# A cross-attention block on one core: context before the low scores, turned weights on two queues, SyncE in written order

## The chip, the cores and the metric

The kernel runs on one core of one Trainium2 chip, as one launch. The time is in device microseconds (us). The core has TensorE (PE; its weight loads are shown as PEld), VectorE (DVE), ScalarE (ACT), GpSimd (POOL), SyncE (SP), which issues transfers, and 16 DMA engines that move them. ScalarE has a DMA queue of its own (ACTq), SyncE another (SPq). Issuing a transfer takes time on the engine that issues it.

## The reference

One transformer block with cross attention, in float32, over 128 sequences of 128 tokens with 256 features; 16 heads of 16, a hidden layer of 1024. `query` is x, `key` and `values` are both the context. Token i sees context tokens j < i, so token 0 sees nothing and its attention weights are set to zero.

```python
q = (query @ Wq + bq)...; k = (key @ Wk + bk)...; v = (values @ Wv + bv)...   # split into 16 heads
scores = jnp.einsum('bhqd,bhkd->bhqk', q, k) / jnp.sqrt(jnp.float32(D_K))
allowed = j < i + mask                                   # mask = 0
scores = jnp.where(allowed, scores, NEG_INF)
attn = jax.nn.softmax(scores, axis=-1)
attn = attn.at[:, :, 0, :].set(0.0)
ctx = jnp.einsum('bhqk,bhkd->bhqd', attn, v)
attn_out = ctx @ Wo + bo
x = layer_norm(query + attn_out, ln1_g, ln1_b)
ffn = jax.nn.relu(x @ W1 + b1) @ W2 + b2
out = layer_norm(x + ffn, ln2_g, ln2_b)
```

## The kernel before

The 128 sequences are taken two at a time: 64 pairs, numbered p. Loop step p (L790) is a software pipeline over four pairs. It makes the scores and the softmax of pair p, the attention output and first normalization of pair p - 1, the hidden layer of pair p - 2 and the second product of pair p - 3, and it projects queries, keys and values of pair p + 1. Pairs 0 and 1 are done ahead of the loop, steps 2 to 5 have a filling order of their own (`plan`), and the last step and the lines after the loop drain it.

Tokens 64 to 127 of a sequence are called high and see up to 128 context tokens; tokens 0 to 63 are low and see at most 64. `scores` makes 32 small matmuls (32 rows, 64 columns of the array) for each part, with 256 streamed columns for high and 128 for low, into the two PSUM buffers of `ps_2`, which both parts use in turn. `mask` (VectorE) reads them from there, in two halves for each part, so a part's scores wait for the masks of the part before. Then the softmax passes between engines: `maximum` (VectorE, then a subtraction on GpSimd, L354), `exponential` (ScalarE, L361), `sums` (VectorE, then a multiplication on GpSimd, L375). The high part goes through maximum, exponential and sums in two halves of eight heads (ONE and TWO), the low part at once (ALL).

To multiply with the values, the weights have to be turned. `turn` transposes 32 x 32 blocks on VectorE into `tb` (three instructions, two for high and one for low), and 16 transfers on SyncE's queue (L401, 96 KB each) bring the blocks to their partitions in `pT`. Both tiles have one buffer. `weigh(p)` multiplies `pT` with the values (96 small matmuls, 128 rows and 32 columns, into `pc`; L434, L444), `context` copies the result (ScalarE, L456), `attention_out` multiplies with Wo. `turn_x1` turns the normalized x in the same way, by five transfers through DRAM (`x1t`, `x1T`), for `hidden`. Before `weigh`, `values_out` (ScalarE) copies the values to `vz` and sends a part of them by a transfer of its own to `vd` (L305).

The bank pool `ps_1` has four PSUM buffers, used in the order py (second product), pc, pq (queries), po (attention output), pk (keys), pv (values), and four ph (hidden, two chunks of the hidden layer each). `hidden` is evicted by ScalarE (`hT`, L615, two instructions for each ph); `second` makes 16 matmuls for each sequence of the pair. `finish`, `norm2` and `store` complete the second normalization, one step later.

The order on PE, DVE, ACT and POOL is the order in which the lines are written (`manual_schedule`, L60). SyncE's order is left to the framework, which interleaves loads and other transfers as it plans them. In the written order of one step TensorE does: high scores, second product of the first sequence, low scores, second product of the second sequence, weigh, queries, attention output, keys, values, hidden. Loads of the transposed blocks `xb` and `cb` (four transfers for two pairs) and of the tokens `x` (three buffers) stand near the end of a step (L843).

Each transfer signals one of eight semaphores, which the framework gives out in turn over both queues; a transfer waits until the earlier one with the same semaphore has landed, where that is not known already.

Of the kernel before, what the change touches and what calls it, by code (L numbers as in the profile page):

```python
# [8 lines left out]
F32 = mybir.dt.float32  # L9
# [4 lines left out]
P = 128  # L14
# [5 lines left out]
def tile_cross_attention_block(  # L20
# [36 lines left out]

    ET = mybir.EngineType
    ctx.enter_context(
        tc.manual_schedule(engines={ET.PE, ET.DVE, ET.Activation, ET.Pool})  # L60
    )

    const = ctx.enter_context(tc.tile_pool(name="const", bufs=1))
# [16 lines left out]
    def load(ps, both="xc"):  # L80

        n = len(ps)
        for which in both:
            src = x if which == "x" else c
            t = loads.tile(
                [P, KC, n * 2 * NS, 32], F32, tag=f"{which}b{n}", name=f"{which}b_{ps[0]}",
                bufs=n,
            )
            blocks = src[2 * ps[0] : 2 * ps[0] + 2 * n].rearrange(
                "b (i t) (k j f) -> j t k (b i) f", t=32, k=KC, f=32  # L90
            )
            for j in range(NS):
                nc.sync.dma_start(t[32 * j : 32 * j + 32], blocks[j])  # L93
            for u, p in enumerate(ps):
                blocks_of[which, p] = t[:, :, u * 2 * NS : (u + 1) * 2 * NS]

    def load_tokens(g, us=slice(0, 4)):
        if g not in tokens_of:
            tokens_of[g] = loads.tile([P, 4, D], F32, tag="x", name=f"x_{g}")
        nc.sync.dma_start(  # L100
            tokens_of[g][:, us], x[4 * g + us.start : 4 * g + us.stop].rearrange("b p d -> p b d")
        )
# [162 lines left out]
    def queries(p):  # L265
        st = states[p]
        st["qT"] = proj.tile([P, KC, TP], F32, tag="qT", name=f"qT_{p}")
        pq = project(wq, st["xT"], f"pq_{p}")
        for m in range(KC):
            nc.scalar.activation(  # L270
                st["qT"][:, m, :], pq[:, m * TP : (m + 1) * TP], AF.Identity,
                bias=bqs_c[:, m : m + 1], scale=QSCALE,
            )
# [41 lines left out]
    def scores(p, hi):  # L315

        st = states[p]
        n = P if hi else HP
        sps = [pair(f"pss{hi}_{p}_{t}") for t in range(2)]
        for m in range(KC):  # L320
            for s in range(2):
                first = s * P
                for r in range(NS):
                    strip = slice(32 * r, 32 * r + 32)
                    nc.tensor.matmul(  # L325
                        sps[r // 2][
                            s * HP : (s + 1) * HP, r % 2, m * 2 * n : (m + 1) * 2 * n
                        ].rearrange("p (e j) -> p e j", e=2),
                        st["qT"][strip, m, first + hi * HP : first + hi * HP + HP],
                        st["kT"][strip, m, :, first : first + n],  # L330
                        start=True, stop=True,
                    )
        st["sps", hi] = sps
        st["sm", hi] = soft.tile([P, H, n], F32, tag=f"sm{hi}", name=f"sm{hi}_{p}")
        st["nmx", hi] = small.tile([P, H], F32, tag=f"nmx{hi}", name=f"nmx{hi}_{p}")
# [43 lines left out]

    def turn(p):


        st = states[p]
        tb = soft.tile([P, NS, (H + HH) * 32], F32, tag="tb", name=f"tb_{p}")
        at = 0
        for hi in (1, 0):
            sm = st["sm", hi].rearrange("p h j -> p (h j)")
            for t in range(sm.shape[1] // 1024):  # L390
                nc.vector.transpose(  # L391
                    tb[:, :, at : at + 256].rearrange("p j (n a) -> p n j a", a=32),
                    sm[:, t * 1024 : (t + 1) * 1024].rearrange(
                        "p (n j a) -> p n j a", j=NS, a=32
                    ),
                )
                at += 256
        pT = soft.tile([P, NS, (H + HH) * 32], F32, tag="pT", name=f"pT_{p}")
        for i in range(NS):
            for j in range(NS):  # L400
                nc.sync.dma_start(  # L401
                    pT[32 * j : 32 * j + 32, i, :], tb[32 * i : 32 * i + 32, j, :]
                )
        st["pT"] = pT.rearrange("p i (n a) -> p i n a", a=32)

    def turn_on_pe(p, hi, ts):

# [63 lines left out]
    def stats(p, t, i):  # L471
        st = states[p]
        mv = st["mv", i] = small.tile([P, 2, 2], F32, tag=f"mv{i}", name=f"mv{i}_{p}")
        for s in range(2):
            bs = small.tile([P, 6], F32, tag="bs", name=f"bs{i}_{p}_{s}", bufs=4)
            nc.vector.bn_stats(bs, t[:, s])
            nc.vector.bn_aggr(mv[:, s], bs)
# [8 lines left out]
    def attention_sum(p):  # L486
        st = states[p]
        t1 = st["t1"] = ffn.tile([P, 2, D], F32, tag="t1", name=f"t1_{p}")
        nc.vector.tensor_tensor(
            t1, st.pop("po").rearrange("p (s d) -> p s d", s=2), st.pop("xb"), ALU.add  # L490
        )
        stats(p, t1, 1)
        deviation(p, 1)

    def norm1(p):
# [102 lines left out]
        for k in range(KC):  # L598
            nc.scalar.copy(st["x1T"][:, :, :, k, :], pt[:, k])  # L599

    def hidden(p, fs):
        st = states[p]
        if fs[0] == 0:
            st["hT"] = ffn.tile([P, FC, TP], F32, tag="hT", name=f"hT_{p}")
        for f in fs[::2]:
            ph = bank(f"ph_{p}_{f}")
            for i in range(2):
                for k in range(KC):
                    nc.tensor.matmul(  # L609
                        ph[:, i * TP : (i + 1) * TP].rearrange("p (s i a) -> p s i a", s=2, a=32),  # L610
                        w1[:, k, (f + i) * P : (f + i + 1) * P], st["x1T"][:, :, :, k, :],
                        start=(k == 0), stop=(k == KC - 1),
                    )
            for i in range(2):
                nc.scalar.activation(  # L615
                    st["hT"][:, f + i, :], ph[:, i * TP : (i + 1) * TP], AF.Relu,
                    bias=b1e_c[:, f + i : f + i + 1], scale=1.0,
                )

    def second(p, s, fs=range(FC)):  # L620
        st = states[p]
# [136 lines left out]
    attention_out(0)  # L758
    exponential(1, 1, TWO)
    attention_sum(0)  # L760
    queries(2)
    sums(1, 1, ONE)
    norm1(0)
# [7 lines left out]
    for which in "xc":  # L771
# [14 lines left out]
        4: ([("hidden", 2, 0)], [("hidden", 2, 1)], [("second", 2, 0)]),  # L786
        5: ([("second", 2, 1)], [("hidden", 3, 0)], [("hidden", 3, 1)]),
    }
    waiting, late = [], []
    for p in range(2, NP):  # L790
        soon, end = p + 1 < NP, p == NP - 1
        first, then, finally_ = plan.get(
            p, ([("second", p - 3, 0)], [("second", p - 3, 1)], both("hidden", p - 2))
        )
        scores(p, 1)
        mask(p, 1, 0)
        maximum(p, 1, ONE)
        feed(first)
        mask(p, 1, 1)
        maximum(p, 1, TWO)  # L800
        scores(p, 0)
        mask(p, 0, 0)
        mask(p, 0, 1)
        exponential(p, 1, ONE)
        maximum(p, 0, ALL)
        exponential(p, 1, TWO)
        feed(then)
        sums(p, 1, ONE)
        sums(p, 1, TWO)
        summed = late + sum_up(first + then)  # L810
        exponential(p, 0, ALL)
        sums(p, 0, ALL)
        for q in waiting:
            finish(q)
        weigh(p - 1)
        context(p - 1)
        if soon:
            queries(p + 1)
        attention_out(p - 1)
        if not end:  # L820
            turn(p)
        attention_sum(p - 1)
        if soon:
            keys(p + 1)
        if p + 2 < NP:
            for which in "xc":
                tokens(p + 2, which)
        norm1(p - 1)
        if p > 4:
            turn_x1(p - 1)  # L830
        if soon:
            values(p + 1)
            values_out(p + 1)
        for q in waiting:
            store(q)
        if p == 2:
            turn_x1_on_pe(p - 1)
        residual1(p - 1)
        for q in summed:
            stats(q, states[q]["t2"], 2)  # L840
        if soon:
            add_bo(p + 1)
        if p % 2 == 0 and p + 4 < NP:  # L843
            load([p + 4, p + 5], "x")
            load_tokens(p // 2 + 2)
        if p % 2 == 1 and p + 3 < NP:
            load([p + 3, p + 4], "c")
        for q in summed:
            scale_and_shift(q)
        feed(finally_)  # L850
        if end:
            turn_on_pe(p, 1, range(4))
        if p in (3, 4):
            turn_x1_on_pe(p - 1)
        late = sum_up(finally_)
        for q in summed:
            norm2(q)
        waiting = summed
# [9 lines left out]
    attention_out(p)  # L868
    second(p - 2, 1, range(FC // 2, FC))
    attention_sum(p)  # L870
    second_sum(p - 2)
    hidden(p - 1, range(FC))
    norm1(p)
# [72 lines left out]
```

## Time and profile before

The profiled execution is one run, taken by the hardware profiler.

| What | Value |
|---|---|
| Median of 3 runs | 1624.45 us (1621.69 to 1626.28) |
| Profiled execution | 1624.0 us, span 1622.2 us, granted TensorE clock 0.997 |
| Busy: PE, PEld | 1602.6 us (99%), 1338.3 us (83%) |
| Busy: DVE, POOL, ACT | 1315.3 us (81%), 1274.9 us (79%), 765.6 us (47%) |
| Chain that ended last | PE 94% |
| pT transfers on SyncE's queue | 976, each 96.0 KB, 2.1 us from issue to landing |
| One steady step | 24.61 us, the same for p = 6 to 61 within 0.01 |

A busy share is the part of the span in which an engine had an instruction running. Matmuls are pipelined and overlap each other, so a busy PE may still be waiting for a short time; the chain of waits gives the time from stage to stage. In a timeline or a chain row, the first number is the start from the span's begin, the second the time it covers, x the number of instructions that are merged in it; brackets hold the idle time before it and what ended it. In a windows row, the last two numbers are the busy share of the DMA engines and the rate in GB/s.

### The profile page before, as it was taken

The numbers are of one execution on the slowest core, as the hardware profiler recorded it, in microseconds if no ns is written. First come the engines' busy times: TensorE is split into PE (matmuls) and PEld (weight loads), VectorE is DVE, ScalarE is ACT, GpSimd is POOL, SyncE is SP. The second block draws the span as 40 slices with busy tenths as digits, with TensorE's granted clock in tenths as the row PEclk, the third lists the DMA queues.
The fourth block names the chain that finished last, engine by engine and source line by source line (L and its number), as shares of the span: only waits on it lengthen the run. The fifth ranks groups of instructions, "written<-read, shape, count | busy, mean of one in ns | idle before, by whom it ended". The sixth has DMA issues, their size and how long they took to land.

```text
span 1622.2 us, 41250 instructions
## 1 busy us (share of the span) xinstructions
PE 1602.6 (99%) x16532; PEld 1338.3 (83%) x16532; DVE 1315.3 (81%) x1988; ACT 765.6 (47%) x1500; POOL 1274.9 (79%) x1105
## 2 busy tenths in 40 slices
PE   8999999999999999999999999999999999999998
PEld 6788888888888888888888888888888888888887
DVE  5789788888888888888888888888888888888852
ACT  4544444544444544444444445445444444445442
POOL 5788787887887887887887878878878878878882
PEclk9999999999999999999999999999999999999999
DMA  9345655656565665665565555566656656556430
GB/s 182 70 102 125 141 130 132 136 130 144 133 138 128 135 139 138 133 131 133 131 145 133 132 136 131 131 144 137 135 131 133 139 138 133 129 134 133 112 82 27
DMA packets 479998, 208.80 MB, mean 129 GB/s; under 512 B 352064, under 2 KB 448320, under 8 KB 479808
## 3 DMA queue, kind: packets, MB, share of 16 engines
q1 hardware_dynamic: 394864, 181.24, 50.2%
q10 hardware_dynamic: 84944, 24.92, 6.5%
q8 instruction: 132, 2.16, 0.6%
q14 instruction: 58, 0.48, 0.1%
HBM read 69.48 MB, written 32.24 MB: 63 GB/s over the span
## 4 chain that ended last, share of the span: by engine, by line
PE 94%; SPq 3%; DVE 1%; DMA 1%; issue 1%; POOL 0%; ACT 0%; POOLq 0%; ACTq 0%; DVEq 0%
PE py L625 27%; PE ph L609 26%; PE pq L259 7%; PE po L463 7%; PE pss L325 7%; PE pk L259 7%; PE pv L291 6%; PE pc L444 3%; PE pc L434 2%; SPq L401 1%; SPq L93 1%; PE py L637 1%; DVE sm L342 1%; DVE nmx L353 0%; PE ptp L417 0%
## 5 line engine op out<-in xcount | busy, mean ns | idle before, releaser
L354 POOL TENSOR_TENSOR sm<-sm,nmx 128x1024 f32<-128x1024 f32 x192 | 364.5, 1899 | 189.2 <-DVE nmx L353 185.8
L609 PE MATMUL ph<-x1T,w 128*128 128x256 f32 x2048 | 454.1, 379 | 2.1 <-ACT x1T L599 2.1
L625 PE MATMUL py<-w,hT 128*128 128x256 f32 x1952 | 453.6, 385 | 0.0
L609 PEld LDWEIGHTS ph<-x1T,w 128*128 128x128 f32 x2048 | 388.5, 190 | 56.8 <-ACT x1T L599 3.2
L625 PEld LDWEIGHTS py<-w,hT 128*128 128x128 f32 x1952 | 361.0, 190 | 76.9 <-ACT hT L615 21.9
L342 DVE TENSOR_TENSOR sm<-pss,neg 128x1024 f32<-128x1024 f32 (+1 forms) x256 | 237.7, 949 | 190.4 <-PE pss L325 190.4
L361 ACT ACTIVATE sm<-sm 128x1024 f32<-128x1024 f32 x192 | 203.0, 1058 | 342.5 <-POOL sm L354 342.4
L375 POOL TENSOR_TENSOR sm<-sm,rs 128x1024 f32<-128x1024 f32 x192 | 359.4, 1901 | 2.8 <-DVE rs L374 2.8
L615 ACT ACTIVATE hT<-ph,b1e_c 128x256 f32<-128x256 f32 x512 | 214.4, 471 | 184.7 <-PE ph L609 149.9
L391 DVE STREAM_TRANSPOSE tb<-sm 128x1024 f32<-128x1024 f32 x183 | 220.4, 1230 | 33.1 <-POOL sm L375 23.8
L353 DVE TENSOR_REDUCE nmx<-sm 128x8 f32<-128x1024 f32 (+1 forms) x192 | 234.2, 1220 | 6.6
L373 DVE TENSOR_REDUCE su<-sm 128x8 f32<-128x1024 f32 (+1 forms) x192 | 229.5, 1195 | 1.1 <-ACT sm L361 0.8
L281 ACT ACTIVATE kT<-pk,bkh,half 128x256 f32<-128x256 f32 x256 | 123.8, 565 | 160.4 <-PE pk L259 160.4
L325 PE MATMUL pss<-kT,qT 32*64 32x256 f32 (+1 forms) x4096 | 127.7, 334 | 5.7 <-DVE sm L342 3.4
L259 PE MATMUL pq<-xT,wq 128*128 128x256 f32 x512 | 129.6, 397 | 0.0
L463 PE MATMUL po<-wo,cxT 128*128 128x256 f32 x512 | 122.9, 384 | 1.4 <-ACT cxT L456 1.4
L509 POOL TENSOR_TENSOR x1b<-x,g_r 128x512 f32<-128x512 f32 x64 | 81.5, 1274 | 53.6 <-DVE x L501 53.6
L291 PE MATMUL pv<-wv,cT 128*128 128x256 f32 x512 | 121.0, 379 | 0.0
L259 PE MATMUL pk<-cT,wk 128*128 128x256 f32 x512 | 121.0, 379 | 0.0
L325 PEld LDWEIGHTS pss<-kT,qT 32*64 32x64 f32 x4096 | 76.5, 131 | 53.6 <-issue 41.8
L463 PEld LDWEIGHTS po<-wo,cxT 128*128 128x128 f32 x512 | 98.2, 192 | 15.4 <-ACT cxT L456 1.6
L259 PEld LDWEIGHTS pk<-cT,wk 128*128 128x128 f32 x512 | 97.4, 190 | 13.3
(86 smaller groups left out, 1687.6 us busy)
## 6 DMA issues: line engine op xcount, KB each, us to landing
pT<-tb SPq DMA_DIRECT2D x976, 96.0 KB, 2.1
out_dram<-t ACTq DMA_DIRECT2D x63, 256.0 KB, 4.1
xb<-in_x_dram SPq DMA_DIRECT2D x124, 128.0 KB, 4.4
cb<-in_ctx_dram SPq DMA_DIRECT2D x124, 128.0 KB, 4.4
x<-in_x_dram SPq DMA_DIRECT2D x31, 512.0 KB, 4.3
x1t<-tbx SPq DMA_DIRECT2D x236, 64.0 KB, 1.8
x1T<-x1t SPq DMA_DIRECT2D x59, 256.0 KB, 3.1
vd<-vz ACTq DMA_DIRECT2D x64, 128.0 KB, 3.6
```

What stands on the lines that cost most here:

```text
L259: nc.tensor.matmul(ps[:, m * TP : (m + 1) * TP], w[:, k, m * P : (m + 1) * P], src[:, k, :], start=(k == 0), stop=(k == KC - 1),)
L291: nc.tensor.matmul(pv[:, s * D : (s + 1) * D], st["cT"][:, k, s * P : (s + 1) * P], wv[:, k, :], start=(k == 0), stop=(k == KC - 1),)
L325: nc.tensor.matmul(sps[r // 2][s * HP : (s + 1) * HP, r % 2, m * 2 * n : (m + 1) * 2 * n].rearrange("p (e j) -> p e j", e=2), st["qT"][str ...
L342: nc.vector.tensor_tensor(st["sm", hi][:, part, :].rearrange("p (r n) j -> p r n j", r=2), st["sps", hi][t][:, :, : 4 * n].rearrange("p r ...
L353: nc.vector.tensor_reduce(nmx[:, part], sm[:, part, :], AX.X, ALU.max, negate=True)
L354: nc.gpsimd.tensor_tensor(sm[:, part, :], sm[:, part, :], nmx[:, part, None].to_broadcast([P, part.stop - part.start, n]), ALU.add,)
L373: nc.vector.tensor_reduce(su, sm[:, part, :], AX.X, ALU.add)
L375: nc.gpsimd.tensor_tensor(sm[:, part, :], sm[:, part, :], rs[:, :, None].to_broadcast([P, part.stop - part.start, n]), ALU.mult,)
L391: nc.vector.transpose(tb[:, :, at : at + 256].rearrange("p j (n a) -> p n j a", a=32), sm[:, t * 1024 : (t + 1) * 1024].rearrange("p (n j ...
L463: nc.tensor.matmul(po[:, s * D : (s + 1) * D], cxT[:, k, s, :], wo[:, k, :], start=(k == 0), stop=(k == KC - 1),)
L609: nc.tensor.matmul(ph[:, i * TP : (i + 1) * TP].rearrange("p (s i a) -> p s i a", s=2, a=32), w1[:, k, (f + i) * P : (f + i + 1) * P], st[ ...
L625: nc.tensor.matmul(st["py"][:, s * D : (s + 1) * D], st["hT"][:, f, s * P : (s + 1) * P], w2[:, f, :], start=(f == 0), stop=(f == FC - 1),)
```

## The change

The change gives steps 7 to 62 a written order of their own, `steady(p)`; the other steps keep theirs.

- On TensorE a steady step does: high scores, both halves of the second product, weigh, low scores, queries, attention output, keys, values, hidden.
- `turn` is split into its three transposes. In a steady step the two high ones follow the low maximum, the low one follows the statistics of the first normalization and the transposition of the next x block.
- `bring` issues the 16 pT transfers. In a steady step SyncE issues the first eight behind the last transpose, and ScalarE issues the other eight between the evictions of `hidden`: none after the first pair of evictions, two after the second, two after the third, four after the fourth.
- `attention_sum` leaves its statistics to `attention_stats`, which comes later in a steady step. The sum of the second product stands between the two high sums on VectorE.
- SyncE joins the written order (`ET.SP`). The loads stand at the head of a step (`load_ahead`), and the tokens have two buffers instead of three.

```diff
-        tc.manual_schedule(engines={ET.PE, ET.DVE, ET.Activation, ET.Pool})
+        tc.manual_schedule(engines={ET.PE, ET.DVE, ET.Activation, ET.Pool, ET.SP})
...
-            tokens_of[g] = loads.tile([P, 4, D], F32, tag="x", name=f"x_{g}")
+            tokens_of[g] = loads.tile([P, 4, D], F32, tag="x", name=f"x_{g}", bufs=2)
...
-    def turn(p):
...
+    def turn(p, hi, t):
...
+        at = (t if hi else 2) * 256
+        nc.vector.transpose(
+            st["tb"][:, :, at : at + 256].rearrange("p j (n a) -> p n j a", a=32),
...
+    def bring(p, queue, which):
...
+        for u in which:
+            i, j = u // NS, u % NS
+            queue.dma_start(
+                st["pT whole"][32 * j : 32 * j + 32, i, :], st["tb"][32 * i : 32 * i + 32, j, :]
+            )
...
-    def hidden(p, fs):
+    def hidden(p, fs, between=None):
...
+            if between:
+                between(f)
...
+    def load_ahead(p):
+        if p % 2 == 0 and p + 4 < NP:
+            load([p + 4, p + 5], "x")
+        if p % 2 == 1 and p + 3 < NP:
+            load([p + 3, p + 4], "c")
+            load_tokens((p + 3) // 2)
+
+    def steady(p):
+
+        nonlocal waiting, late
+        scores(p, 1)
+        mask(p, 1, 0)
+        maximum(p, 1, ONE)
+        second(p - 3, 0)
+        mask(p, 1, 1)
+        maximum(p, 1, TWO)
+        exponential(p, 1, ONE)
+        second(p - 3, 1)
+        if p + 2 < NP:
+            tokens(p + 2, "c")
+        sums(p, 1, ONE)
+        exponential(p, 1, TWO)
+        summed = late + sum_up(both("second", p - 3))
+        sums(p, 1, TWO)
+
+
+        weigh(p - 1)
+        context(p - 1)
+        scores(p, 0)
+        queries(p + 1)
+        mask(p, 0, 0)
+        mask(p, 0, 1)
+        maximum(p, 0, ALL)
+        exponential(p, 0, ALL)
+        turn(p, 1, 0)
+        turn(p, 1, 1)
+        for q in waiting:
+            finish(q)
+        attention_out(p - 1)
+        attention_sum(p - 1)
+        sums(p, 0, ALL)
+        attention_stats(p - 1)
+        if p + 2 < NP:
+            tokens(p + 2, "x")
+        turn(p, 0, 0)
+        bring(p, nc.sync, range(NS * NS // 2))
+        keys(p + 1)
+        norm1(p - 1)
+        turn_x1(p - 1)
+        values(p + 1)
+        values_out(p + 1)
+        for q in waiting:
+            store(q)
+        add_bo(p + 1)
+        residual1(p - 1)
+        for q in summed:
+            stats(q, states[q]["t2"], 2)
+        for q in summed:
+            scale_and_shift(q)
+        at = NS * NS // 2
+
+        def share(f):
+            nonlocal at
+            n = 0 if f == 0 else NS if f == FC - 2 else NS // 2
+            bring(p, nc.scalar, range(at, at + n))
+            at += n
+
+        hidden(p - 2, range(FC), share)
+        late = []
+        for q in summed:
+            norm2(q)
+        waiting = summed
...
+        load_ahead(p)
+        if p > 6 and not end:
+            steady(p)
+            continue
...
-        if p % 2 == 0 and p + 4 < NP:
-            load([p + 4, p + 5], "x")
-            load_tokens(p // 2 + 2)
-        if p % 2 == 1 and p + 3 < NP:
-            load([p + 3, p + 4], "c")
```

More of the change, by code (lines that the diff above doesn't have):

```diff
@@ L378, in sums @@
         )
-    def turn(p):
+    def turn(p, hi, t):
         st = states[p]
[L386 to L404, printed above, removed]
+        if "tb" not in st:
+            st["tb"] = soft.tile([P, NS, (H + HH) * 32], F32, tag="tb", name=f"tb_{p}")
+        at = (t if hi else 2) * 256
+        nc.vector.transpose(
+            st["tb"][:, :, at : at + 256].rearrange("p j (n a) -> p n j a", a=32),
+            st["sm", hi].rearrange("p h j -> p (h j)")[:, t * 1024 : (t + 1) * 1024].rearrange(
+                "p (n j a) -> p n j a", j=NS, a=32
+            ),
+        )
+    def bring(p, queue, which):
+        st = states[p]
+        if "pT" not in st:
+            pT = st["pT whole"] = soft.tile([P, NS, (H + HH) * 32], F32, tag="pT", name=f"pT_{p}")
+            st["pT"] = pT.rearrange("p i (n a) -> p i n a", a=32)
+        for u in which:
+            i, j = u // NS, u % NS
+            queue.dma_start(
+                st["pT whole"][32 * j : 32 * j + 32, i, :], st["tb"][32 * i : 32 * i + 32, j, :]
+            )
     def turn_on_pe(p, hi, ts):
@@ L491, in attention_sum, with attention_stats @@
         )
-        stats(p, t1, 1)
+    def attention_stats(p):
+        stats(p, states[p]["t1"], 1)
         deviation(p, 1)
@@ L760, in tile_cross_attention_block @@
     attention_sum(0)
+    attention_stats(0)
     queries(2)
@@ L820, in tile_cross_attention_block @@
         if not end:
-            turn(p)
+            turn(p, 1, 0)
+            turn(p, 1, 1)
+            turn(p, 0, 0)
+            bring(p, nc.sync, range(NS * NS))
         attention_sum(p - 1)
+        attention_stats(p - 1)
         if soon:
@@ L870, in tile_cross_attention_block @@
     attention_sum(p)
+    attention_stats(p)
     second_sum(p - 2)
```

## The prediction

> **What bounds the kernel now.** I read four views. The page's first table gives the engine that has no room, and the chain of waits in one steady step (780 to 880 us) gives its stages.
>
> ```profile
> PE 1602.6 (99%) x16532; PEld 1338.3 (83%) x16532; DVE 1315.3 (81%) x1988; ACT 765.6 (47%) x1500; POOL 1274.9 (79%) x1105
> ```
>
> ```profile
> 807.64 6.91 PE ph L609 x32
> 814.54 1.05 PE pss L325 x32
> 815.59 3.65 PE py L625 x16
> 819.24 0.77 PE pss L325 x30
> 820.01 3.65 PE py L625 x16
> 823.66 0.36 PE pc L434 x16
> 824.02 0.45 PE pc L444 x32
> 824.47 0.22 PE pc L434 x16
> 824.70 0.45 PE pc L444 x32
> 825.14 1.93 PE pq L259 x8
> 827.07 1.73 PE po L463 x8
> ```
>
> The chain is TensorE alone: the step from one ph row to the next is 24.61 us, and every steady step repeats it. Only fewer TensorE microseconds per step, or a new wait, can move the end. The rows also price a change of tile shape. A full-size matmul costs 6.91/32 = 0.216, so 16 of them are 3.45, but py shows 3.65: 0.20 for coming from a small shape. pq (1.93 against po's 1.73) pays the same 0.20. Of the small rows, pc pays 0.14 on entry (0.36 against 0.22), and the high scores pay 1.05 - 4 x 0.216 = 0.19 (four rounds of 256 columns).
>
> Next the timeline of that step, for what stands round TensorE.
>
> ```profile
> 808.45 0.60 ACTq L305 DMA_DIRECT2D vd<-vz  x1
> 809.17 0.72 ACTq L545 DMA_DIRECT2D out_dram<-t  x1
> 809.94 0.84 ACT L615 ACTIVATE hT<-ph,b1e_c 128x256 f32<-128x256 f32 x2 [0.48 <-issue]
> 816.18 1.09 ACT L530 ACTIVATE t<-t,nb,sd 128x256 f32<-128x256 f32 x2 [0.76 <-POOL nb L522]
> 818.06 1.21 DVE L342 TENSOR_TENSOR sm<-pss,neg 128x1024 f32<-128x1024 f32 x1
> 819.17 0.84 PE L325 MATMUL pss<-kT,qT 32*64 32x128 f32 x32
> 820.16 1.06 ACT L361 ACTIVATE sm<-sm 128x1024 f32<-128x1024 f32 x1 [2.88 <-POOL sm L354]
> ```
>
> ScalarE stands still while its sequencer issues a transfer (0.48 idle, "issue"). The low scores begin at 819.17, but the second high mask, which frees the bank that they also write, ends at 818.06 + 1.21 = 819.27. Four rounds of 128 columns plus entry should be 4 x 0.108 + 0.19 = 0.62; the chain shows 0.77. So 0.15 of it is a wait for that mask, in every step. The idle column does not show it, because the first matmuls count as busy meanwhile.
>
> Last, SyncE's own waits and the transfers:
>
> ```profile
> SPq L401 <- DMA vd<-vz: 104.2, 56, 3.2
> ```
>
> ```profile
> L401 SPq DMA_DIRECT2D pT<-tb x20: 507/590/1252, 807.3 to 833.8; - x20
> DMA to landing us min/median/max: 2.0/2.2/3.0
> ```
>
> A pT issue on SyncE waited for ScalarE's vd: the two queues share eight completion semaphores, and each transfer waits for the one eight places before it.
>
> **The change, part by part** (56 steps, p = 7 to 62; times T from a step's first high-score matmul, 814.47 in this trace).
>
> *Context, then low scores, behind the second product.* Before: py, low scores, py, pc = 3.65 + 0.77 + 3.65 + 1.48 = 9.55. After, both py halves stand together: 32 x 0.216 + 0.20 = 7.10. pc keeps 1.48, since it still comes from a full shape. The low scores are free of the mask (it ends at T 4.8, they start at 9.6): 0.62. pq still comes from a small shape. The sum is 9.20, that is 0.35 less. The unknown term is the switch from pc's shape to the scores', for which no row exists. The Trainium skill (TensorEngine Tiling (Array Packing), Key Properties) says that a change of tiling mode, not just of tile, drains the engine. With that, this boundary costs what pq pays, 0.15 from the last small start to the next first start; without it, the 0.04 between groups of pc; at most the 0.31 from a full matmul to a small one. I take 0.15: it is also small work that drains. Per step the saving is 0.35, between 0.19 and 0.46; a step becomes 24.26. Times 56: 19.6 us, between 10.6 and 25.8.
>
> *VectorE and GpSimd.* The same instructions in another order; what matters is whether the end of a step still comes in time. Low scores end near T 10.4. VectorE: masks and maximum 2.45 (12.85), two turns of the high part 2.33, attention_sum 0.66. GpSimd subtracts meanwhile (1.90) and ScalarE exponentiates (1.06), so the low sums run 15.95 to 17.45. GpSimd's multiply 1.90 ends at 19.4, the last turn (1.25) at 20.7. Then norm1, turn_x1 and two stats, 2.55: VectorE is done at 23.3, and its next mask is due at 24.26 + 1.2. Some 2 us of cover. GpSimd's last nb ends near 26.3, its next subtraction is due at 28.0. second_sum now waits for py's end (T 8.3), with only the second sums and the low masks behind it, and those need the scores at 10.4 anyway. norm1 behind the last turn delays x1T, which hidden needs a full step later.
>
> *SyncE.* Eight pT transfers instead of sixteen, four x1t, one x1T, then the loads (4, or 5 in an odd step). By rows: 8 x 0.64 + 4 x 0.49 + a landing of 2 + 0.4 + 2.9 to 4.9, some 14 of 24.26 us. Loads now stand behind x1T's wait, but they are needed a step or more later. x1T lands near T 9 of the next step, hidden wants it at 17.3. Token buffers fall from three to two: the wait for add_bo of the step before is past by then. This part costs nothing; without that cover a late load would hold tokens on VectorE.
>
> *Eight pT transfers on ScalarE.* The part with a price. Each holds ScalarE 0.60 to 0.72 (rows vd and out); I take 0.65. Here the order is: kT to 17.9, vz, vd, store to 20.05, hT pairs as ph lets them (19.2, 20.9, 22.65, 24.4). The two transfers after the second pair start at 21.45 (tb is ready at 20.7), the next two at 23.25; pairs end at 20.95, 21.8, 23.6 and 25.45. The next second wants the last hT near 26.8: 1.3 us of cover. Queued behind are the last four transfers, norm2, and then the next step's first exponential, which before started at T 5.69 and so is due at 29.95. By the changed program's instruction order the eighth ScalarE transfer waits for SyncE's eighth in even steps and its seventh in odd ones. That closes a loop from exponential to exponential: 1.1 (exp), 13.7 (sums, second_sum, sums, masks, maximum, turns, attention_sum, low sums, multiply, turn), 7 or 6 issues of c on SyncE, a landing L, 0.65, norm2 1.09 and small gaps: 16.7 + 6.5c + L. c is 0.64 (590 ns plus gap) to 0.87 (the pT issues that stand beside the store took 0.81 and 0.83); two pT issues at once are in no row, and I take 0.70. L is 2.0 to 3.0; with two queues I take 2.5. The loop is 23.75, under 24.26: hidden by 0.5. Its ends are 22.9 and 25.4.
>
> Here a rule speaks against the two queues: the Trainium skill (DMA: Bandwidth & Descriptors, "Issuing engines are not separate DMA queues") says that issuing from several engines saves only issue time. While pT alone was issued, the windows read:
>
> ```profile
> 814.00:815.00 1.00, 1.00 (x26) 0.59 (x32) 0.00 (x0) 0.42 (x2) 0.98 (x2) 1.00 0.65 154
> ```
>
> 0.65 of the DMA engines at 154 GB/s, so 237 GB/s at most, and 16 x 98,304 bytes need 6.6 us. By the row, eight issues each would bring all from 20.7 to some 28.5. By the rule it could be 27.3 at the earliest, plus x1t's share. The next weigh is at 24.26 + 8.15 = 32.4, so both leave pT hidden; the rule's price sits in L, and is why I took 2.5.
>
> *Start, end.* Steps 2 to 6 and 63 keep their order; only loads move. Nothing, within 2 us.
>
> **Sum.** The profiled execution took 1624.0 us (span 1622.2); 1624.0 - 19.6 = 1604.4. It stands 0.45 below the median of the runs, so against 1624.45: **1605**.
>
> **Rivals.**
> 1. *A new loop sets the step* (slower). From 6.5c + L = 7.6 on the loop exceeds 24.26, from 7.9 on the old 24.61. c = 0.82 with L = 2.9 gives 24.9, 0.3 a step over before: 1624 + 17 = 1641; at the far end, 25.4, 1668. For it: issues beside another queue's did stretch, and engines at 0.65 from one queue have no room for two. Against it: only seven issues count, and beside vd they stayed at 0.59.
> 2. *The loop or ScalarE's lateness takes part of the gain*: steps of 24.35 to 24.55, 1610 to 1621.
> 3. *The reordering does not do what it says*: the new switch costs 0.31 and the low scores keep 0.77. Then 0.04 a step is left, 1622. Against it: high scores without such a mask show 0.19 over their columns, not 0.34.
>
> **How the numbers follow.** Fed throughout: 0.64, range of its own 1599 to 1614. Part of the gain lost: 0.13. Nothing gained: 0.07, mostly within 0.3% (5 us, about what a measurement of this kernel tells from no change). The loop sets the step: 0.16, all but 0.02 of it clearly slower. Faster 0.79, same 0.07, slower 0.14. The range reaches from the first case's low end to 1625, which leaves out the slower rival and little else: 1598 to 1625.
>
> **What would show it.** Right: ph rows 24.26 apart; one py row of 32 at 7.10; pss behind pc at 0.62; hT's last pair ends before py asks for it; the first exponential waits for GpSimd, not for issues. Wrong: PEld of py waiting for hT; the exponential with "issue" before it; pT on ScalarE's queue waiting for pT on SyncE's; a pss of 0.77 or more behind pc.

## The result

| | before | after |
|---|---|---|
| Median | 1625.37 us (1621.69 to 1626.83, 4 runs) | 1606.32 us (1604.98 to 1608.22, 4 runs) |
| Ratio | | 0.9887, 95% interval 0.9866 to 0.9908 |
| Profiled execution, its span | 1624.0, 1622.2 us | 1605.48, 1603.8 us |
| Granted TensorE clock | 0.997 | 0.997 |

The change saves 19.05 us; 19.6 were predicted, and 1605 us against the measured 1606.32. First the page of the changed kernel: the engines' table and the two queues' pT transfers (number, size, median us from issue to landing).

```profile
PE 1583.8 (99%) x16532; PEld 1335.0 (83%) x16532; DVE 1367.9 (85%) x1988; ACT 758.8 (47%) x1500; POOL 1282.8 (80%) x1105
...
pT<-tb SPq DMA_DIRECT2D x528, 96.0 KB, 2.8
pT<-tb ACTq DMA_DIRECT2D x448, 96.0 KB, 2.7
```

TensorE still bounds, with 18.8 us less of busy time; a pT transfer lands after 2.7 to 2.8 us where it took 2.1. The chain of waits in one steady step (start, us, what):

```profile
804.86 1.05 PE pss L325 x32
805.91 7.10 PE py L630 x32
813.01 0.36 PE pc L435 x16
813.37 0.45 PE pc L445 x32
813.82 0.22 PE pc L435 x16
814.04 0.45 PE pc L445 x32
814.49 0.62 PE pss L325 x32
815.11 1.92 PE pq L259 x8
```

7.10 + 1.48 + 0.62 = 9.20 is the predicted sum to the hundredth, against 9.55 before. From the first high score (804.86) to the next one the step is 24.26, within 0.01, in all steps but four, which are named below. The boundary that no row of before showed, context to low scores, costs what was taken for it: pc is 1.48 long ahead of the scores, as it was ahead of the queries.

The other thing to read is ScalarE, in the timeline of the same step:

```profile
807.03 2.40 ACTq L403 DMA_DIRECT2D pT<-tb  x3
809.54 1.09 ACT L533 ACTIVATE t<-t,nb,sd 128x256 f32<-128x256 f32 x2 [3.30 <-DMA pT<-tb]
810.54 1.04 ACT L361 ACTIVATE sm<-sm 128x1024 f32<-128x1024 f32 x1
812.86 1.06 ACT L361 ACTIVATE sm<-sm 128x1024 f32<-128x1024 f32 x1 [1.27 <-POOL sm L354]
```

norm2 (L533) waits 3.30 us behind the last pT issues, which wait for a transfer. The first exponential (L361) follows with no idle time, at T 5.75 (T counted from the first matmul's record, 804.79), where the forecast had it due at T 5.69. It is 0.06 late, and nothing follows from that: the second exponential stands at T 8.07, as in the steps where the first is on time. How much cover this loop has is worked out further below. Over the whole run ScalarE waited like this for 104.6 + 40.8 us, and TensorE felt little of it (6.9 us of py's weight loads waited for hT; it was 21.9 before):

```profile
ACT t L533 <- DMA pT<-tb: 104.6, 32, 4.3
ACT hT L618 <- DMA pT<-tb: 40.8, 19, 3.4
PEld py L630 <- ACT hT L618: 6.9, 18, 0.4
```

Between 975 and 1122 us the cover was gone. The six steps there took 24.31, 24.43, 24.27, 24.73, 24.26 and 25.15, together 1.6 us more than six of 24.26. The chain of the worst one:

```profile
1096.64 1.71 SPq L403
1098.35 0.04 issue
1098.39 0.59 SPq L403
...
1100.30 3.15 DMA pT<-tb
1103.45 0.02 issue
1103.47 2.08 DMA pT<-tb
1105.55 0.24 issue
1105.79 0.32 PE pc L435 x8
```

The first exponential of the step that these issues belong to was already 1.6 late (T 7.29), and one pT issue on SyncE took 1.71 us instead of 0.59. ScalarE's last issue (1103.47) followed the landing of SyncE's last transfer (1103.45), and the weigh of the next step waited for what it brought.

### The profile page after: what moved, and what is told of

Same layout as the page of the kernel before. It is cut to its first block, busy times and chain, and to the rows that moved or that the text cites. A ratio compares the mean times of both kernels' runs of the same rounds, so it can differ in the third digit from the quotient of the medians.

```text
span 1603.8 us, 41273 instructions
## 1 busy us (share of the span) xinstructions
PE 1583.8 (99%) x16532; PEld 1335.0 (83%) x16532; DVE 1367.9 (85%) x1988; ACT 758.8 (47%) x1500; POOL 1282.8 (80%) x1105
## 4 chain that ended last, share of the span: by engine, by line
PE 93%; DVE 2%; DMA 1%; SPq 1%; issue 1%; POOL 1%; ACT 1%; POOLq 0%; ACTq 0%; DVEq 0%
PE ph L612 26%; PE py L630 25%; PE pq L259 8%; PE po L464 7%; PE pk L259 7%; PE pv L291 7%; PE pss L325 6%; PE pc L445 3%; PE pc L435 2%; SPq L403 1%; DVE sm L342 1%; DMA pT<-tb 1%; DVE nmx L353 1%; PE ptp L418 0%; PE py L642 0%
## 5 line engine op out<-in xcount | busy, mean ns | idle before, releaser
L630 PE MATMUL py<-w,hT 128*128 128x256 f32 x1952 | 438.8, 382 | 0.0
L375 POOL TENSOR_TENSOR sm<-sm,rs 128x1024 f32<-128x1024 f32 x192 | 364.1, 1900 | 76.4 <-DVE rs L374 73.1
L630 PEld LDWEIGHTS py<-w,hT 128*128 128x128 f32 x1952 | 365.6, 190 | 70.4 <-issue 16.3
L361 ACT ACTIVATE sm<-sm 128x1024 f32<-128x1024 f32 x192 | 201.4, 1054 | 211.4 <-POOL sm L354 211.2
L373 DVE TENSOR_REDUCE su<-sm 128x8 f32<-128x1024 f32 (+1 forms) x192 | 233.5, 1216 | 56.2 <-ACT sm L361 52.7
L533 ACT ACTIVATE t<-t,nb,sd 128x256 f32<-128x256 f32 x124 | 67.7, 593 | 181.9 <-DMA pT<-tb 104.6
L325 PE MATMUL pss<-kT,qT 32*64 32x256 f32 (+1 forms) x4096 | 118.9, 335 | 5.0 <-issue 3.2
L270 ACT ACTIVATE qT<-pq,bqs_c 128x256 f32<-128x256 f32 x128 | 53.7, 471 | 126.1 <-PE pq L259 126.1
L259 PEld LDWEIGHTS pq<-xT,wq 128*128 128x128 f32 x512 | 94.7, 195 | 21.5 <-issue 9.9
```

What stands on the lines that cost most here:

```text
L259: nc.tensor.matmul(ps[:, m * TP : (m + 1) * TP], w[:, k, m * P : (m + 1) * P], src[:, k, :], start=(k == 0), stop=(k == KC - 1),)
L325: nc.tensor.matmul(sps[r // 2][s * HP : (s + 1) * HP, r % 2, m * 2 * n : (m + 1) * 2 * n].rearrange("p (e j) -> p e j", e=2), st["qT"][str ...
L373: nc.vector.tensor_reduce(su, sm[:, part, :], AX.X, ALU.add)
L375: nc.gpsimd.tensor_tensor(sm[:, part, :], sm[:, part, :], rs[:, :, None].to_broadcast([P, part.stop - part.start, n]), ALU.mult,)
L630: nc.tensor.matmul(st["py"][:, s * D : (s + 1) * D], st["hT"][:, f, s * P : (s + 1) * P], w2[:, f, :], start=(f == 0), stop=(f == FC - 1),)
```

## The experiments

Each is compared with the kernel before, measured beside it (medians 1623.47 and 1623.53 us in the two sets of runs).

**1. The mask's wait alone (mask_free).** The kernel before, with the low scores four of sixteen matmuls later, where the second high mask is past (its expectation calls the four matmuls two groups).

```diff
+        part = p > 5
+        if part:
+            second(p - 3, 1, range(2))
         scores(p, 0)
...
-        feed(then)
+        if part:
+            second(p - 3, 1, range(2, FC))
+        else:
+            feed(then)
```

> The kernel before with one edit: from p = 6 on, the low scores stand behind the first two of sixteen matmul groups of the second product's second half, so that the second high mask is past when they start. The number of changes of tile shape stays the same. Theory (0.15 of the 0.77 us of the low scores is a wait for that mask, and part of the change's gain comes from it): the low scores take 0.62 from start to start, the step falls from 24.61 to 24.46 us, 58 steps give 8.7 us: about 1616 us. Rival (0.77 is what these matmuls cost behind a full shape, and the change gains only from shapes): 24.61 us, about 1625.

Measured: 1633.77 us, ratio 1.0066 (1.0052 to 1.0079). Ten us slower, where the theory had 8.7 us less and the rival no change. From the chain of waits:

```profile
805.24 1.92 PE pq L259 x8
807.17 0.02 issue
807.19 1.99 PE po L463 x8
...
820.60 4.51 PE py L625 x20
825.11 0.62 PE pss L325 x32
825.73 2.79 PE py L625 x12
```

The low scores did fall to 0.62. But po (here that of the step before) rose from 1.73 to 1.99, and the waits say why:

```profile
PEld po L463 <- ACT cxT L456: 26.0, 57, 2.1
```

In the kernel before this wait was there once (1.6 us), here in 57 steps, 0.46 each as the weight loads count it. The timeline of ScalarE has the place:

```profile
830.37 1.06 ACT L361 ACTIVATE sm<-sm 128x1024 f32<-128x1024 f32 x1 [1.77 <-POOL sm L354]
831.33 0.56 ACT L456 COPY cxT<-pc 128x508 f32<-128x508 f32 x1
```

The low exponential stands ahead of the context copy in the written order. Scores that end 0.7 later make that exponential 0.36 later (T 10.89 instead of 10.53). The copy ends at 831.89, po's first matmul would be due at 830.00 + 1.92 = 831.92, and its weight loads, which run ahead of the matmuls, have to wait. The step becomes 24.75: 0.15 won, 0.29 lost. 58 x 0.14 is 8; 10 were measured. The profiled execution is 11.2 longer than that of before: 8.1 in steps 7 to 62, 1.8 from the start of step 63 on, 1.2 ahead of step 7.

**2. The same, with the context ahead of the low exponential (context_ahead).**

```diff
+        if part:
+            weigh(p - 1)
+            context(p - 1)
         exponential(p, 0, ALL)
         sums(p, 0, ALL)
         for q in waiting:
             finish(q)
-        weigh(p - 1)
-        context(p - 1)
+        if not part:
+            weigh(p - 1)
+            context(p - 1)
```

> The last kernel with low scores moved behind two matmul groups of the second product was slower, though its low scores took 0.62 as expected: TensorE waited for cxT in attention output (0.3 to 0.4 a step), because on ScalarE the copy of the context stands behind the low exponential, and that now came 0.3 later. This kernel adds one edit: from p = 6 on, weigh and context stand ahead of the low exponential, as in the changed kernel. Theory (the wait for the mask is worth 0.15 a step, but only where the low exponential no longer stands ahead of the context): low scores 0.62, attention output starts without a wait, step 24.46, 58 steps: 8.7 us less than before, 1614 to 1617. Rival (moving the low scores costs as much as the wait, whatever the order on ScalarE): 1622 us or more.

Measured: 1615.62 us, ratio 0.9947 (0.9935 to 0.996). Every steady step is 24.46, and ScalarE now has:

```profile
821.73 0.58 ACT L456 COPY cxT<-pc 128x508 f32<-128x508 f32 x1 [1.47 <-PE pc L444]
822.21 1.06 ACT L361 ACTIVATE sm<-sm 128x1024 f32<-128x1024 f32 x1
```

So the wait for the mask is worth 7.9 us, as a size that was predicted (0.15 a step), but in these two kernels it came only with an order on ScalarE that copies the context first. The change has that order, because it writes context ahead of the low softmax.

**3. SyncE's order, early loads and two token buffers alone (sync_order).**

```diff
-engines={ET.PE, ET.DVE, ET.Activation, ET.Pool})
+engines={ET.PE, ET.DVE, ET.Activation, ET.Pool, ET.SP})
...
+tag="x", name=f"x_{g}", bufs=2)
...
+        if p % 2 == 0 and p + 4 < NP:
+            load([p + 4, p + 5], "x")
+        if p % 2 == 1 and p + 3 < NP:
+            load([p + 3, p + 4], "c")
+            load_tokens((p + 3) // 2)
         scores(p, 1)
```

> The kernel before with the third part of the change alone: SyncE in the written order, the loads at the head of a step, two token buffers; the 16 transfers of the turned weights stay on SyncE. Theory (this part costs and brings nothing): 1625 us, within 2 us, step 24.61. Rival (part of the gain comes from SyncE's order): 1607 to 1616 us.

Measured: 1624.36 us, ratio 1.0004 (0.9994 to 1.0014). This part costs nothing and brings nothing.

**4. All but TensorE's order (low_between).** The changed kernel, with the low scores back between the halves of the second product.

```diff
         exponential(p, 1, ONE)
+        scores(p, 0)
         second(p - 3, 1)
...
         context(p - 1)
-        scores(p, 0)
         queries(p + 1)
```

> The changed kernel with the low scores put back between the two halves of the second product on TensorE, in steps 7 to 62; the order on the other engines, both queues, SyncE's order and the loads stay as changed. Theory (all of the gain is TensorE's: one change of tile shape and the wait for the mask): low scores 0.77 again, two rows of second product of 3.65, step 24.61, 1623 to 1626 us, as before. Rival (part of the gain comes from the order on the other engines or from the second queue): below 1620.

Measured: 1624.74 us, ratio 1.0004 (0.9995 to 1.0013). Every steady step is 24.61 again, but for three at 1061 to 1161 us (24.80, 25.00 and 25.37, together 1.3 us longer), where the first exponential is late as in the changed kernel. The chain is that of before:

```profile
816.45 3.65 PE py L630 x16
820.10 0.77 PE pss L325 x30
820.87 3.65 PE py L630 x16
```

The whole gain is in where TensorE makes the low scores. All other parts of the change are there in this kernel, and they are worth nothing by themselves.

**5. One queue (one_queue).** They may still be needed. Here SyncE brings all sixteen blocks.

```diff
-        bring(p, nc.sync, range(NS * NS // 2))
+        bring(p, nc.sync, range(NS * NS))
...
-        hidden(p - 2, range(FC), share)
+        hidden(p - 2, range(FC))
```

> The changed kernel with all 16 transfers of the turned weights on SyncE, where its eight stood; ScalarE issues none. All else is kept. Theory (the second queue is needed to pay for the later low scores): the turned weights are ready to bring at T 21.0 of a step, 16 issues of 0.63 us and a landing of 2.1 to 2.8 us bring the last at 33.1 to 33.8, while the weigh wants them at 32.4 (T 8.15 of the next step); the buffer of the transposed blocks is free only then, so that the step becomes a loop of weigh to low scores to turn to weigh of 24.8 to 25.1 us: 1635 to 1651 us, slower than before. Rival (a second issuing engine brings no bandwidth, and the transfers are hidden anyway): 24.26 a step, about 1606.

Measured: 1654.67 us, ratio 1.0199 (1.0181 to 1.0217). Slower than before by 31 us, with steady steps from 24.26 to 26.26, 25.16 on the mean. SyncE's row in the timeline, and TensorE's in the middle of a weigh:

```profile
824.98 10.72 SPq L403 DMA_DIRECT2D pT<-tb  x16
```

```profile
810.61 0.32 PE L435 MATMUL pc<-pT,vd 128*32 128x64 f32 x8
812.29 0.32 PE L435 MATMUL pc<-pT,vd 128*32 128x64 f32 x8 [1.36 <-DMA x1t<-tbx]
```

Sixteen issues take 10.72 us from T 22.5 on, and the weigh stops after eight matmuls until the second sequence's blocks are there. (The wait is put down to x1t, the next transfer on that queue, since it came last; what these matmuls read is pT.) So TensorE waits where the theory had it wait. The time lies 4 us over the expected upper end: over all steps an issue took 0.67 on the mean, where 0.63 was taken.

**6. Ten and six (ten_six).** Two issues behind each of the last three pairs of evictions.

```diff
-        bring(p, nc.sync, range(NS * NS // 2))
+        bring(p, nc.sync, range(10))
...
-        at = NS * NS // 2
+        at = 10
...
-            n = 0 if f == 0 else NS if f == FC - 2 else NS // 2
+            n = 0 if f == 0 else 2
```

> The changed kernel with ten transfers of the turned weights on SyncE and six on ScalarE, two behind each of the last three pairs of evictions; so none of ScalarE's waits for one of SyncE's late ones. Theory (the loop from exponential to exponential through ScalarE's last transfers lies just under the step, and made the six longer steps of the changed kernel): the first exponential at T 5.7 in every step, norm2 near T 26.5 and not 28.3 to 29.0, every steady step 24.26, 1604 to 1605 us. Rival (the loop has nothing to do with the longer steps): they come again, 1606 us. Second rival (ten issues on SyncE bring the last too late for the weigh: 21.0 + 10 x 0.63 + 2.8 = 30.1 against 32.4): steps above 24.26.

Measured: 1604.11 us, ratio 0.9884 (0.9868 to 0.9899). Every steady step is 24.26, with no longer one among them, and the first exponential stands at T 5.69 in all of them:

```profile
809.07 1.09 ACT L533 ACTIVATE t<-t,nb,sd 128x256 f32<-128x256 f32 x2 [1.38 <-POOL nb L525]
812.43 1.06 ACT L361 ACTIVATE sm<-sm 128x1024 f32<-128x1024 f32 x1 [2.27 <-POOL sm L354]
```

norm2 waits for GpSimd's nb, not for a transfer, and ends 2.3 us before the exponential is due. The longer steps at 975 to 1122 us are gone, so they came from the loop. The median is 2.2 us under the changed kernel's, but the kernel before was 1.9 us faster in this set too, and the ratios (0.9884 and 0.9887) are the same within their intervals; it is the trace that tells the two kernels apart, not the time.

**7. Two microseconds more on ScalarE (extra_two, ten_six_two).** The same addition to the changed kernel and to the last one.

```diff
+    spare_in = const.tile([P, 960], F32, tag="spare_in", name="spare_in")
+    nc.gpsimd.memset(spare_in, 1.0)
+    spare_out = const.tile([P, 960], F32, tag="spare_out", name="spare_out")
...
         for q in summed:
             norm2(q)
+        nc.scalar.copy(spare_out, spare_in)
+        nc.scalar.copy(spare_out, spare_in)
         waiting = summed
```

> The changed kernel with two copies of 960 elements behind norm2 on ScalarE in every steady step, 2.0 to 2.2 us in all; what they copy is not used. ScalarE's eighth transfer waits here for SyncE's sixth or seventh. Theory (the loop from exponential to exponential lies just under the step, so 2 us more on ScalarE come through): the loop's mean is some 23.3 without the copies, 25.3 to 25.6 with them, the first exponential waits for transfers and not for GpSimd, step near 25.4: 1655 to 1680 us. Rival (ScalarE is 47% busy and has room for 2 us): 24.26 a step, 1604 to 1607.

> The same two unused copies behind norm2, in the kernel with ten transfers on SyncE and six on ScalarE. Theory (there the loop is open, because ScalarE's last transfer waits for none of SyncE's late ones): norm2 at T 26.6 to 27.7, copies to 29.8, first exponential due at 29.95: 24.26 a step, 1603 to 1608. Rival (2 us more on ScalarE cost whatever the queues do): as the kernel with eight and eight and the copies, 1640 or more.

Measured: eight and eight 1671.35 us, ratio 1.0289 (1.0275 to 1.0303), mean step 25.39; ten and six 1606.28 us, ratio 0.9889 (0.9875 to 0.9902), every step 24.26. ScalarE's timeline of the first, and then of the second:

```profile
812.64 1.09 ACT L537 ACTIVATE t<-t,nb,sd 128x256 f32<-128x256 f32 x2 [3.29 <-DMA pT<-tb]
813.64 0.98 ACT L870 COPY spare_out<-spare_in 128x960 f32<-128x960 f32 x1
814.64 0.99 ACT L871 COPY spare_out<-spare_in 128x960 f32<-128x960 f32 x1
815.54 2.00 ACT L365 ACTIVATE sm<-sm 128x1024 f32<-128x1024 f32 x2
```

```profile
810.03 1.09 ACT L537 ACTIVATE t<-t,nb,sd 128x256 f32<-128x256 f32 x2 [1.38 <-POOL nb L529]
811.03 0.98 ACT L870 COPY spare_out<-spare_in 128x960 f32<-128x960 f32 x1
812.03 0.99 ACT L871 COPY spare_out<-spare_in 128x960 f32<-128x960 f32 x1
813.39 1.06 ACT L365 ACTIVATE sm<-sm 128x1024 f32<-128x1024 f32 x1 [0.36 <-POOL sm L358]
```

The same 1.97 us cost 65 us in one kernel and, within the measurement, nothing in the other. An engine that is busy for 47% of the span had no room for 2 us, because a wait for another queue's transfers stood in its order ahead of them. In the first kernel both high exponentials start late and as one row of two: they are the tail of the loop, and the next turns hang on them.

## Why the prediction was right, and where it was not

**TensorE's sum: right.** 0.35 a step was predicted, 24.61 to 24.26 was measured. Its two parts have a run each: 0.15 for the wait (experiment 2, steps of 24.46) and 0.20 for one change of shape less (from there to 24.26; py is 4.51 + 2.79 = 7.30 there and 7.10 in the changed kernel). The switch from context to low scores was bounded by 0.04 and 0.31; the rule of the Trainium skill (TensorEngine Tiling (Array Packing), Key Properties), by which the value 0.15 was chosen, gave the measured one: pc's 1.48 did not change. The trace agrees with the rule; it does not show the draining itself.

**"The low scores are free of the mask": right in size, with a condition that was not named.** The prediction counted the 0.15 as free once the mask is past. Experiment 1 shows that being past the mask is not enough: the low exponential must also stand behind the context copy on ScalarE, or po gives it all back and more. The change meets this condition, so the number held; the step of the prediction followed TensorE and VectorE, but not which ScalarE instruction stands ahead of cxT.

**SyncE's part costs nothing: right** (experiment 3).

**VectorE: covered, but with about half the cover.** The last turn was predicted to end at T 20.7; it ends at 20.96. What follows it was put at 2.55 and takes 3.33, so that VectorE is done at T 24.29, not 23.3, and waits 1.16 us for the next scores where some 2 were forecast:

```profile
825.67 1.61 DVE L504 TENSOR_SCALAR x<-t,mv,sd 128x256 f32<-128x256 f32 x2
830.25 1.23 DVE L342 TENSOR_TENSOR sm<-pss,neg 128x1024 f32<-128x1024 f32 x1 [1.16 <-PE pss L325]
```

The mis-sized term is norm1 (L504): its first instruction takes 1.29 us in the steady steps, 0.41 before. GpSimd's addition of xb now runs beside it (825.54 to 826.81) and did not before; whether that is the cause was not tested.

**The loop: the mechanism right, but its terms are not constant.** From exponential to the last turn 14.8 us were worked out, and in the steps where the loop binds it is 14.81. For what follows the turn, here is a quiet step (52, which starts at 1267.37):

```profile
1288.42 5.02 SPq L403 DMA_DIRECT2D pT<-tb  x8
1293.90 2.38 ACTq L403 DMA_DIRECT2D pT<-tb  x3
1296.38 1.09 ACT L533 ACTIVATE t<-t,nb,sd 128x256 f32<-128x256 f32 x2 [3.28 <-DMA pT<-tb]
1297.38 1.04 ACT L361 ACTIVATE sm<-sm 128x1024 f32<-128x1024 f32 x1
```

The last turn ends at 1288.35, and the exponential starts 9.03 later. (A first exponential that is on time leaves 0.46 of waits for others on the way: from T 5.69 to 20.96 are 15.27. Only when it is later than that does the last turn move.) With 14.81 the loop is 23.84, and 23.18 in the odd steps, which have one issue less in it: 23.5 on the mean, where 23.75 was forecast. An issue took 0.63 here (0.70 taken), ScalarE's last issue 0.52 (0.65 taken), and the landing that it waits for 2.9 (2.5 taken): two terms too large and one too small. The quiet cover was 0.75 us and not 0.5. Experiment 7 bears this out: in the quiet steps of its first kernel (49 to 56) a step is 25.03; less the 1.9 that the copies take this is a loop of 23.1, and one issue less than 23.5 is 22.9 (its ScalarE waits for a transfer that is one place earlier).

What the forecast lacked is that issues and landings are slower in some stretches. In steps 37 to 48, at 900 to 1190 us, seven issues took 4.9 to 6.1 us instead of 4.4, and from step 36 to 46 the loop took 24.55 on the mean, in two of them over 25.4. There it was longer than the step, which is rival 2 for a few steps and cost 1.6 us. In steps 13 to 21 the first exponential slid as well, to T 6.68, and TensorE lost nothing. The profiled execution fits: 56 x 0.345 is 19.3, less 1.6 is 17.7; 18.5 were measured, 0.7 of them ahead of step 7.

**Two of the signs failed.** The prediction listed "pT on ScalarE's queue waiting for pT on SyncE's" as a sign of being wrong, and an exponential that waits for GpSimd as a sign of being right. Here the waits came and the forecast held, because they end just in time. A better sign would have been the offset of the first exponential within its step: 5.7 is hidden, and TensorE of the changed kernel lost time only from about 7.5 on. A third sign, py's weight loads waiting for hT, could not tell: it was there before the change, and longer (21.9 us, now 6.9).

**Rival 1** (the loop sets the step) did not come, but it is real: 2 us more on ScalarE brought it in experiment 7. **Rival 3** (0.77 kept, switch at 0.31) is excluded by the rows.

**The rule on issuing engines.** The Trainium skill's "Issuing engines are not separate DMA queues" (DMA: Bandwidth & Descriptors) says that a second issuing engine saves only issue time. This agrees with the traces, and here issue time was what counted: sixteen issues on one queue were 10.7 us and made the kernel slower by 31 us, while with two queues each landing took 0.6 to 0.7 longer (2.2 us with one queue in experiment 5, 2.7 and 2.8 with two), so they do share what moves the data. How the transfers are split matters as well: ten and six leaves the loop open.

## What to carry to other kernels

A gain on the bounding engine is worked out from its rows, but each instruction that is moved on it also moves its readers: look at what stands ahead of the next needed result on the evicting engine before the gain is booked. When an engine issues transfers, look up which earlier transfer each issue has to wait for; that wait holds everything behind it in the engine's order, and can close a loop over a whole step. The distance of such a loop to the step is the number to work out, and an added microsecond on the suspected engine measures it.

## What was not expected of the hardware

Two queues that issue 96 KB transfers at once do not slow each other's issues in most steps (0.63 us a piece, as with one), only their landing (2.1 to 2.7 and 2.8). But there are stretches of 200 to 300 us in which the issues are slower. In the changed kernel a pT issue on SyncE takes 0.60 us on the mean at 550 to 900 us, 0.72 at 900 to 1200 (up to 1.78), and 0.60 after that. The second queue does not bring these stretches: in the kernel before, with one, the mean is 0.60 at 550 to 750 us, 0.66 at 750 to 950, and 0.60 at 1000 to 1300. The kernel with ten and six has one too (0.57 at 550 to 850 us, 0.65 at 850 to 1200), without harm, and in the one with the low scores between the halves the first exponential slides to T 8.4 at about 1061 us. That the steps of the changed kernel are longer there because of the loop is shown by experiment 6; what slows the issues is open.
